# Graph norm and attention on one core: row sums of the attention weights by adding transfers in place of TensorE, with the finishing steps put in other places

## The chip, the cores and the metric

The kernel runs on one core of one Trainium2 chip. The metric is device time in microseconds; before the change it is 2455.19 us, the median of three runs (2455.09 to 2455.25). All data is float32.

## What is computed

Two layers. The first is a graph convolution with two matrix products and batch norms; the second is an attention whose queries come from a graph product and whose keys and values come from the rows themselves. The change touches the end of the second layer only: the softmax's denominators and what divides by them.

```python
# layer 1, cut (x: 16 batches of 1024 rows of 256; h = 4 heads of hd = 64)
Wg = adj[None, :, :] * A_s                              # A_s from the rows' means
g = jnp.einsum('bcn,bnm->bcm', fea, Wg)
g = jax.nn.relu(g * para.reshape(1, C, N))
q = jnp.transpose(g, (0, 2, 1)).reshape(B, N, h, hd).transpose(0, 2, 1, 3)
kv = (x @ kv_w).reshape(B, N, 2, h, hd).transpose(2, 0, 3, 1, 4)
k, v = (kv[0], kv[1])
attn = jax.nn.softmax(jnp.einsum('bhnd,bhmd->bhnm', q, k) * scale, axis=-1)
out = jnp.einsum('bhnm,bhmd->bhnd', attn, v)
# ...
x = _layernorm(x + out, axis=-1)
```

The kernel takes the softmax apart: it computes the exponentials e of the scores without a maximum, sums e times v over the keys, sums e over the keys for the denominator, and divides at the very end, when the rows are finished.

## The kernel before

The kernel computes the attention in steps. A step is two blocks of 128 keys for one pair of heads and one half (512) of the queries. Four steps make a turn: one pair, one half of a batch. Four turns make a batch, in the order half 0 pair 0, half 0 pair 1, half 1 pair 0, half 1 pair 1. In each step TensorE makes the scores of the step after, ScalarE the exponentials, VectorE adds them to a running sum, and TensorE multiplies them with the values.

```python
def exps(g):
    for a in range(2):
        E[g, a] = ep.tile([P, 2, FB], F32, tag="e", name=f"e{g}_{a}")
        nc.scalar.activation(E[g, a], S.pop((g, a)), AF.Exp)

def sums(g):
    b, hf, pair, cp = step(g)
    # ... (the very last step is left to dens)
    if cp == 0:
        ACC[b, hf, pair] = accp.tile([P, 2, FB], F32, tag="acc", name=f"acc{g}")
        nc.vector.tensor_add(ACC[b, hf, pair], E[g, 0], E[g, 1])
    else:
        for a in range(2):
            nc.vector.tensor_add(ACC[b, hf, pair], ACC[b, hf, pair], E[g, a])
```

The running sum `acc` has 128 partitions, [128, 2 heads, 512 queries]: each partition holds the sum over every 128th key. What is missing is the sum over the 128 partitions. TensorE makes it after both pairs of a half, by a product with ones, 32 output rows a head, all alike. ScalarE copies the result, and eight rows a head go to a buffer in DRAM beside the heads' outputs:

```python
DR = 8
CD = C + HEADS * DR
# ...
accp = right("accp", 2)
# ...
def dens(b, hf):
    p = ps_t.tile([P, FB], F32, tag="t", name="pd")
    for pair in range(NP):
        acc = ACC.pop((b, hf, pair))
        for h in range(2):
            k = 32 * (2 * pair + h)
            more = EX.get((b, hf, pair), [])
            for n, t in enumerate(more + [acc]):
                nc.tensor.matmul(
                    p[k : k + 32, :], ones32, t[:, h, :], start=n == 0, stop=n == len(more)
                )
    DT[b, hf] = otp.tile([P, FB], F32, tag="dt", bufs=1, name=f"dt{b}_{hf}")
    nc.scalar.copy(DT[b, hf], p)
    if not by_pe(b, hf):
        for k in range(HEADS):
            put_o(b, hf, slice(C + k * DR, C + (k + 1) * DR), DT[b, hf][32 * k : 32 * k + DR, :])
```

The buffer is read back in blocks of 32 rows (`fetch_o`), VectorE transposes these blocks, and so has for each query its 256 outputs and its four denominators in one partition:

```python
def finish_a(b, j):
    # ... (the last half of the last batch takes another way: by_pe)
        t = pool_r[0].tile([P, 2, CD], F32, tag=pool_r[1], name=f"r_{b}_{j}")
        nc.vector.transpose(
            t.rearrange("p a c -> p (a c)"), OB.pop((b, j)).rearrange("p a c -> p (a c)")
        )
        nc.vector.reciprocal(rd, t[:, :, C:].rearrange("p a (h r) -> p a h r", r=DR)[:, :, :, 0])
        p = r = t[:, :, :C]
    # ... times rd, plus the rows of before, mean and variance (VectorE),
    # ... the norm's factors (GpSimd); finish_b applies them (ScalarE) and stores
```

One `finish_a` covers 256 queries, so a half has two and a batch four (j = 0 to 3). The pieces that are not steps are put into the turns by a table: `put(b, t, f, ...)` places f ahead of the steps of turn t // 2 of batch b (t may run on into the next batch), `between` places it after a given step. Within a turn they are ordered by rank:

```python
order = (dens, recips, x1_t, finish_a, fetch_o, finish_b, x1_v, rows, ln1_a, ln1_b, put_x1, get_x1, means, load, crow)
```

`bn2_q` (GpSimd) scales a later batch's fetched rows, `rows` transposes them and adds (VectorE), `ln1_a` takes their mean and variance (VectorE, then GpSimd), `ln1_b` applies the norm (ScalarE), and `x1_v` transposes the normed rows once more (VectorE); `keys`, `values` and `graph` are products on TensorE for the next batch, and `gate` makes the graph's weights (ScalarE, VectorE). The first sum of a turn stands behind the last of the turn's short pieces of TensorE, `dens` among them:

```python
behind = max((k + 1 for k, fa in enumerate(now) if is_short(fa)), default=0)
```

Of the kernel before, what the change touches and what calls it, by code (L numbers as in the profile page):

```python
# [9 lines left out]
F32 = mybir.dt.float32  # L10
AF = mybir.ActivationFunctionType
OP = mybir.AluOpType
# [4 lines left out]
P = 128  # L17
# [5 lines left out]
def gnn_norm_attention_kernel(  # L23
# [59 lines left out]
    y_blk = [yT_all[b].rearrange("i (d e) (q n) -> q e (i d) n", e=Q, q=NQ) for b in range(B)]  # L83


    DR = 8
    CD = C + HEADS * DR
    o_dram = {(b, h): dram.tile([NT // NH, CD, P], F32, name=f"o{b}_{h}") for b in range(B) for h in range(NH)}
    x1_dram = {
# [39 lines left out]
    with ExitStack() as l0:  # L129
# [280 lines left out]
        right = lambda name, bufs: ctx.enter_context(tc.tile_pool(name=name, bufs=bufs, side="right"))  # L410
        keep = right("keep", 1)
        ldp = right("ldp", LDP)
        accp = right("accp", 2)
        RD = keep.tile([P, B * NT + 1, HEADS], F32, name="RD")
        ones32 = keep.tile([P, 32], F32, name="ones32")
        stq = keep.tile([P, 2, C // Q], F32, name="stq")
# [164 lines left out]
    def fast():  # L581
      with ExitStack() as fx:
# [245 lines left out]
        def by_pe(b, hf):  # L828
            return b == B - 1 and hf == NH - 1

        def attend(g):
            b, hf, pair, cp = step(g)
            if cp == 0:
                O[b, hf, pair] = [ps_t.tile([P, FB], F32, tag="t", name=f"o{g}_{r}") for r in range(2)]
            for a in range(2):
                cb = 2 * cp + a
                for r in range(2):
                    for h in range(2):
                        nc.tensor.matmul(  # L839
                            O[b, hf, pair][r][h * HD : (h + 1) * HD, :],  # L840
                            vs[b][r * HD : (r + 1) * HD, cb, pair * P + h * HD : pair * P + (h + 1) * HD],
                            E[g, a][r * HD : (r + 1) * HD, h, :],
                            start=(cb == 0),
                            stop=(cb == NT - 1),
                        )
# [65 lines left out]
        def finish_a(b, j):  # L911
            hf, k = divmod(2 * j, KB)
            pool_r = (rp, "r") if b < B - 1 or not by_pe(b, hf) else (x1p, "x1")
            rd = RD[:, b * NT + 2 * j : b * NT + 2 * j + 2, :]
            if by_pe(b, hf):
                r = pool_r[0].tile([P, 2, C], F32, tag=pool_r[1], name=f"r_{b}_{j}")
                p = OB.pop((b, j))
            else:
                t = pool_r[0].tile([P, 2, CD], F32, tag=pool_r[1], name=f"r_{b}_{j}")
                nc.vector.transpose(  # L920
                    t.rearrange("p a c -> p (a c)"), OB.pop((b, j)).rearrange("p a c -> p (a c)")
                )
                nc.vector.reciprocal(rd, t[:, :, C:].rearrange("p a (h r) -> p a h r", r=DR)[:, :, :, 0])
                p = r = t[:, :, :C]
            if j == NT // 2 - 1 and by_pe(b, hf):

                for a in range(2):
                    for h in range(HEADS):
                        nc.scalar.mul(r[:, a, ts(h, HD)], p[:, a, ts(h, HD)], rd[:, a, h : h + 1])
            else:  # L930
                nc.vector.tensor_mul(
                    r.rearrange("p a (h d) -> p a h d", h=HEADS),
                    p.rearrange("p a (h d) -> p a h d", h=HEADS),
                    rd.unsqueeze(3).to_broadcast([P, 2, HEADS, HD]),
                )
            nc.vector.tensor_add(r, r, x1s.pop((b, j)))
            mv, rs = ln_stats(sm, r, f"z{b}_{j}")
            nm = sm.tile([P, 2], F32, tag="nm", name=f"nm_{b}_{j}")
            for a in range(2):
                nc.gpsimd.tensor_scalar(  # L940
                    nm[:, a : a + 1], mv[:, a, 0:1], rs[:, a : a + 1], -1.0, op0=OP.mult, op1=OP.mult
                )
            R[b, j] = (r, rs, nm)

        def finish_b(b, j):
            r, rs, nm = R.pop((b, j))
# [46 lines left out]
        for b in range(B):  # L993

            for hf in range(NH):
                t = (hf + 1) * (NC // NH)
                put(b, t, dens, b, hf)
                if by_pe(b, hf):
                    put(b, t, recips, b, hf)
                for k in range(KB // 2):  # L1000
                    j = hf * (KB // 2) + k

                    if b * NH + hf < B * NH - 3:
                        t_f, t_a, t_b = (t + 1, t + 2 + k, t + 6 + k) if hf == 0 else (t + 1, t + 4 + k, t + 6 + k)
                    elif not by_pe(b, hf):

                        t_f, t_a, t_b = t, t + 2 * k, t + 2 + 2 * k if b < B - 1 else (t + 2, NC + 1)[k]
                        if b == B - 1 and k == 0:
                            between[(b * NC + t_b) * 2 + NK // 2] = [(finish_b, (b, j))]
                            t_b = None  # L1010
                    else:
                        t_f, t_a, t_b = t, t + 1 + k, t + 2 + k
                    put(b, t_f, back if by_pe(b, hf) else fetch_o, b, j)
                    if t_a == t:
                        between[(b * NC + t) * 2 + NK // 2] = [(finish_a, (b, j))]
                    else:
                        put(b, t_a, finish_a, b, j)
                    if t_b is not None:
                        put(b, t_b, finish_b, b, j)
            if b == 0:  # L1020
                continue

            if b > 1:
                put(b - 2, 2, begin, b)
                for j in range(NT // 2):
                    put(b - 2, j, load, b, j)
                    put(b - 2, j + 1, bn2_q, b, j)
                    put(b - 2, j + 2, rows, b, j)
                    put(b - 2, j + 2, ln1_a, b, j)
                    put(b - 2, j + 3, ln1_b, b, j)  # L1030
                    put(b - 2, j + 3, put_x1, b, j)
                    put(b - 2, 5 + j // 2 * 2, get_x1, b, j)
                    put(b - 2, min(6 + j, NC), x1_v, b, j)
                put(b - 2, NC - 2, means, b)
                put(b - 2, NC - 1, crow, b)

            i = 0
            for t, n in enumerate(WG):
                for i in range(i, i + n):
                    put(b - 1, t, gate, b, i)  # L1040
# [15 lines left out]
        nsteps = B * NS  # L1056


        order = (dens, recips, x1_t, finish_a, fetch_o, finish_b, x1_v, rows, ln1_a, ln1_b, put_x1, get_x1, means, load, crow)
        rank = {f: k for k, f in enumerate(order)}  # L1060
        short = (dens, recips, x1_t, back)

# [15 lines left out]
        def arrange(pieces):  # L1078
            first = []
            gates = [fa for fa in pieces if fa[0] is gate]  # L1080
            many = [fa for fa in pieces if fa[0] in long]
            first += [fa for fa in pieces if fa[0] is bn2_q]
            alone = [fa for fa in pieces if fa[0] in (dens, back, recips, crow)]
            few = [fa for fa in pieces if fa not in first + gates + many + alone]
# [119 lines left out]
        for t in range(-NC // 2, max(max(at) // 2, nsteps // NK - 1) + 1):  # L1204
            g = NK * t
            now = [p for s in (2 * t, 2 * t + 1) for p in [(opening, (s,))] + arrange(at.get(s, []))]
            behind = max((k + 1 for k, fa in enumerate(now) if is_short(fa)), default=0)
            for k in range(len(now) + 1):
                if k == behind and 0 <= g < nsteps:
                    sums(g)  # L1210
                if k < len(now):
                    f, a = now[k]
                    f(*a)
            for k in range(g, g + NK):
                if 0 <= k + 1 < nsteps:
# [174 lines left out]
```

## Time and profile before

| | before |
|---|---|
| time, median of three | 2455.19 us |
| span of the profiled execution | 2454.0 us |
| column sums on TensorE (L870, over `acc`) | 256 instructions, 36.1 us busy |
| ScalarE's copy of them (L874) | 32, 0.586 us each in the median |
| running sums on VectorE (L824) | 382, 1333 ns each |
| transposes of fetched outputs (L920) | 62, 768 ns each |
| GpSimd's scaling of rows (L624) | 120, 1544 ns each |
| transfers | 292.73 MB, 583951 packets, 407528 of them under 512 B |

In the profile, PE is TensorE's matmul, PEld its loading of weights, DVE VectorE, ACT ScalarE, POOL GpSimd and SPq the queue from which transfers are issued. L870 is line 870 of the kernel. A float32 matmul of the program shows as two instructions. The names tell what is written and read: `pd<-acc,ones` is the column sum, `ot<-o,ot` the end of a pair's output, `r<-ob` the transpose of a fetched piece, `e<-s` the exponentials, `yt<-yt,stq` the scaling of rows. In a row of the order of time, the first two numbers are start and length in microseconds, and in square brackets stands how long the engine sat idle before, and for whom. In a row of a group, after the count, stand the busy time in us, the mean length of one in ns, and the idle time before them with what ended it.

### The profile page before, as it was taken

The numbers are of one execution on the slowest core, as the hardware profiler recorded it, in microseconds if no ns is written. First come the engines' busy times: TensorE is split into PE (matmuls) and PEld (weight loads), VectorE is DVE, ScalarE is ACT, GpSimd is POOL, SyncE is SP. The second block draws the span as 40 slices with busy tenths as digits, with TensorE's granted clock in tenths as the row PEclk, the third lists the DMA queues.
The fourth block names the chain that finished last, engine by engine and source line by source line (L and its number), as shares of the span: only waits on it lengthen the run. The fifth ranks groups of instructions, "written<-read, shape, count | busy, mean of one in ns | idle before, by whom it ended". The sixth has DMA issues, their size and how long they took to land. (4 is left out here: it accounts for less than half of the span.)

```text
span 2454.0 us, 33894 instructions
## 1 busy us (share of the span) xinstructions
PE 2411.8 (98%) x12225; PEld 1008.5 (41%) x12225; DVE 1811.3 (74%) x2584; ACT 1094.8 (45%) x1555; POOL 776.9 (32%) x826
## 2 busy tenths in 40 slices
PE   8999999999999899999999999999999999999997
PEld 4444444444344443443434434344343443443432
DVE  5555545556776777888788888888888888888677
ACT  2000000001554455564655646656566565564645
POOL 2222222231556521414224133232332323414013
PEclk9999999999999899999999999999999999999999
DMA  3122122222578543544545545545354453544222
GB/s 137 69 86 103 69 86 103 85 87 86 199 272 278 133 121 83 143 119 112 143 106 129 143 95 146 122 120 144 81 150 114 123 149 89 145 112 118 72 44 56
DMA packets 583951, 292.73 MB, mean 119 GB/s; under 512 B 407528, under 2 KB 556512, under 8 KB 576608
## 3 DMA queue, kind: packets, MB, share of 16 engines
q1 hardware_dynamic: 583776, 290.49, 43.0%
q8 instruction: 98, 1.61, 0.3%
q14 instruction: 77, 0.63, 0.1%
HBM read 194.46 MB, written 95.94 MB: 118 GB/s over the span
## 5 line engine op out<-in xcount | busy, mean ns | idle before, releaser
L809 ACT ACTIVATE e<-s 128x1024 f32<-128x1024 f32 x512 | 496.0, 1020 | 327.5 <-PE s L797 265.4
L824 DVE TENSOR_TENSOR acc<-acc,e 128x1024 f32<-128x1024 f32 x382 | 509.3, 1333 | 112.1 <-ACT e L809 85.4
L797 PE MATMUL s<-qT,kT 64*64 64x512 f32 x4096 | 490.7, 594 | 4.4 <-ACT e L809 1.7
L839 PE MATMUL o<-e,v 64*64 64x512 f32 x4096 | 485.3, 589 | 0.0
L771 PE MATMUL pg<-wg,x 128*128 128x512 f32 x960 | 426.5, 597 | 0.0
L624 POOL TENSOR_TENSOR yt<-yt,stq 128x512 f32<-128x512 f32 x120 | 185.2, 1544 | 406.4 <-DMA yt<-yT 239.8
L771 PEld LDWEIGHTS pg<-wg,x 128*128 128x128 f32 x960 | 178.7, 190 | 238.6 <-issue 237.4
L839 PEld LDWEIGHTS o<-e,v 64*64 64x64 f32 x4096 | 156.6, 133 | 282.9 <-issue 275.2
L797 PEld LDWEIGHTS s<-qT,kT 64*64 64x64 f32 x4096 | 147.1, 133 | 298.5 <-issue 254.2
L107 ACT COPY u<-pa 128x512 f32<-128x512 f32 x15 | 8.8, 586 | 475.3 <-PE pa L313 475.3
L66 POOL TENSOR_SCALAR rs_z<-mv_z 128x2 f32<-128x2 f32 x64 | 18.5, 290 | 470.5 <-DVE mv_z L573 470.4
L730 DVE SCALAR_TENSOR_TENSOR wg<-wg,adj 128x1024 f32<-128x1024 f32 x128 | 163.4, 1308 | 2.8
L313 PE MATMUL pa<-AhT,x 128*128 128x512 f32 x360 | 161.8, 592 | 0.0
L656 ACT ACTIVATE x<-x,nm_a,rs_a 128x256 f32<-128x256 f32 x128 | 75.8, 594 | 171.9 <-POOL nm_a L646 171.4
L851 DVE TENSOR_TENSOR ot<-o,ot 128x512 f32<-128x512 f32 x64 | 44.2, 691 | 127.5 <-ACT ot L850 127.5
L757 PE MATMUL pv<-kvw,x1T 128*128 128x256 f32 x512 | 118.7, 385 | 0.0
L746 PE MATMUL pk<-x1T,kvw 128*128 128x512 f32 x256 | 117.9, 604 | 0.0
L66 POOL TENSOR_SCALAR rs_a<-mv_a 128x2 f32<-128x2 f32 x64 | 38.0, 594 | 236.5 <-DVE mv_a L573 235.2
L344 PE MATMUL ph<-agg,SW 128*128 128x512 f32 x240 | 112.8, 592 | 0.0
L757 PEld LDWEIGHTS pv<-kvw,x1T 128*128 128x128 f32 x512 | 97.1, 192 | 31.8 <-issue 16.2
L313 PE MATMUL pa<-T,sx 128*128 128x512 f32 x240 | 107.9, 592 | 0.0
L313 PEld LDWEIGHTS pa<-AhT,x 128*128 128x128 f32 x360 | 68.4, 190 | 86.1 <-issue 86.1
(198 smaller groups left out, 3147.1 us busy)
## 6 DMA issues: line engine op xcount, KB each, us to landing
adj<-in_adj_dram SPq DMA_DIRECT2D x128, 512.0 KB
h<-hT SPq DMA_DIRECT2D x28, 1024.0 KB
hL<-h SPq DMA_DIRECT2D x28, 1024.0 KB
ob<-o SPq DMA_DIRECT2D x248, 72.0 KB
x<-in_x_dram SPq DMA_DIRECT2D x16, 1024.0 KB
yT<-y SPq DMA_DIRECT2D x64, 256.0 KB
out_dram<-r SPq DMA_DIRECT2D x64, 256.0 KB
xr<-in_x_dram SPq DMA_DIRECT2D x62, 256.0 KB
```

The costliest lines, as they stand in the source:

```text
L313: nc.tensor.matmul(p, xs[n][:, k, :], bs[n][:, k, :], start=(k == 0), stop=(k == KN - 1))
L344: nc.tensor.matmul(p, ws[n][:, ts(f, P)], bs[n], start=True, stop=True)
L624: nc.gpsimd.tensor_tensor(y, y, sc, op)
L656: nc.scalar.activation(r, r, AF.Identity, bias=nm[:, a : a + 1], scale=rs[:, a : a + 1], accum_out=css[b][:, i : i + 1])
L730: nc.vector.scalar_tensor_tensor(t, t, 1.0, adjs[b * NT + i], op0=OP.add, op1=OP.mult)
L746: nc.tensor.matmul(p, kvw[:, k, ts(c, P)], x1Ts[b][:, k, ts(h, FB)], start=(k == 0), stop=(k == CT - 1))
L757: nc.tensor.matmul(p[:, ts(a, C)], x1Ts[b][:, k, ts(j + a, P)], kvw[:, k, C:], start=(k == 0), stop=(k == CT - 1),)
L771: nc.tensor.matmul(pg[b], x1s[b, k // 2][:, k % 2, ts(c, P)], wgs[b, k][:, ts(h, FB)], start=(k == 0), stop=(k == NT - 1))
L797: nc.tensor.matmul(t[r * HD : (r + 1) * HD, h, :], kTs[b, pair][h * HD : (h + 1) * HD, ts(2 * cb + r, HD)], qTs[b, pair, hf][h * HD : (h + ...
L809: nc.scalar.activation(E[g, a], S.pop((g, a)), AF.Exp)
L824: nc.vector.tensor_add(ACC[b, hf, pair], ACC[b, hf, pair], E[g, a])
L839: nc.tensor.matmul(O[b, hf, pair][r][h * HD : (h + 1) * HD, :], vs[b][r * HD : (r + 1) * HD, cb, pair * P + h * HD : pair * P + (h + 1) * HD],
```

## The change

In all half batches but the last three, the sum over the partitions is no longer made by TensorE. Two transfers issued by GpSimd add instead: the first adds partitions 64 to 127 of `acc` to partitions 0 to 63, the second adds 32 to 63 to 0 to 31. The 32 rows that remain, each a sum over every 32nd key, go to DRAM (so 32 rows a head in place of eight), and after the transpose VectorE sums these 32 numbers for each query. The aim is to take the column sums off TensorE and their copy off ScalarE.

For this the running sums get a third buffer, and the pieces are placed anew. The folds stand at the front of the turn after their pair; `put_den` follows within that turn. The second piece of half 1 (`finish_late`) stands behind `ln1_a`, the statistics of later rows; other finishing steps go between steps. Since `dens` no longer holds back the first sum of a turn, a batch's first sum is put behind the transposes of the rows (`x1_v`), which the keys of that turn read. The diff, cut to its core:

```diff
-    DR = 8
+    DR = Q                                   # Q = 32
-        accp = right("accp", 2)
+        accp = right("accp", 3)
+        def by_dma(b, hf):
+            return b * NH + hf < B * NH - 3
+
+        def fold(b, hf, pair, n):
+            acc = ACC[b, hf, pair]
+            nc.gpsimd.dma_start(acc[:n], acc[n : 2 * n], accum_op=OP.add)
+
+        def put_den(b, hf, pair):
+            acc = ACC.pop((b, hf, pair))
+            for h in range(2):
+                r = C + (2 * pair + h) * DR
+                put_o(b, hf, slice(r, r + DR), acc[:DR, h, :])
 ...
-                t = pool_r[0].tile([P, 2, CD], F32, tag=pool_r[1], name=f"r_{b}_{j}")
-                nc.vector.transpose(
-                    t.rearrange("p a c -> p (a c)"), OB.pop((b, j)).rearrange("p a c -> p (a c)")
-                )
-                nc.vector.reciprocal(rd, t[:, :, C:].rearrange("p a (h r) -> p a h r", r=DR)[:, :, :, 0])
-                p = r = t[:, :, :C]
+                p = r = pool_r[0].tile([P, 2, C], F32, tag=pool_r[1], name=f"r_{b}_{j}")
+                den = otp.tile([P, 2, CD - C], F32, tag="den", bufs=1, name=f"den_{b}_{j}")
+                ob = OB.pop((b, j))
+                nc.vector.transpose(den, ob[:, :, C:])
+                nc.vector.transpose(r, ob[:, :, :C])
+                den = den.rearrange("p a (h r) -> p a h r", r=DR)
+                if by_dma(b, hf):
+                    nc.vector.tensor_reduce(rd, den, AX.X, OP.add)
+                    nc.vector.reciprocal(rd, rd)
+                else:
+                    nc.vector.reciprocal(rd, den[:, :, :, 0])
 ...
-                put(b, t, dens, b, hf)
+                if by_dma(b, hf):
+                    for pair in range(NP):
+                        s = b * NC + t + 2 * (pair - NP + 1)
+                        for k in range(2):
+                            put(0, s + k, fold, b, hf, pair, P // 2 >> k)
+                        between.setdefault(2 * s + 2, []).append((put_den, (b, hf, pair)))
+                else:
+                    put(b, t, dens, b, hf)
 ...
                     if b * NH + hf < B * NH - 3:
-                        t_f, t_a, t_b = (t + 1, t + 2 + k, t + 6 + k) if hf == 0 else (t + 1, t + 4 + k, t + 6 + k)
+                        t_f, t_a, t_b = t + 2 + k * hf, t + 3 + hf, t + 6 + k
+                        if k != hf:
+                            t_a = None
+                            between.setdefault((b * NC + t + 2) * 2 + hf, []).append((finish_a, (b, j)))
+                        if hf == 1 and k == 0:
+                            t_f = None
+                            between.setdefault((b * NC + t) * 2 + NK - 1, []).append((fetch_o, (b, j)))
 ...
-                        put(b, t_a, finish_a, b, j)
+                        put(b, t_a, finish_late if by_dma(b, hf) and hf == 1 else finish_a, b, j)
 ...
-        order = (dens, recips, x1_t, finish_a, fetch_o, finish_b, x1_v, rows, ln1_a, ln1_b, put_x1, ...)
+        order = (dens, recips, x1_t, put_den, finish_a, fetch_o, finish_b, x1_v, rows, ln1_a, finish_late, ln1_b, put_x1, ...)
+            first += [fa for fa in pieces if fa[0] is fold]
             first += [fa for fa in pieces if fa[0] is bn2_q]
 ...
-            behind = max((k + 1 for k, fa in enumerate(now) if is_short(fa)), default=0)
+            opens = lambda fa: is_short(fa) or (fa[0] is x1_v and g % NS == 0)
+            behind = max((k + 1 for k, fa in enumerate(now) if opens(fa)), default=0)
```

More of the change, by code (lines that the diff above doesn't have):

```diff
@@ L943, in finish_a, with finish_late @@
             R[b, j] = (r, rs, nm)
+        def finish_late(b, j):
+            finish_a(b, j)
         def finish_b(b, j):
@@ L1008, in fast @@
                         if b == B - 1 and k == 0:
-                            between[(b * NC + t_b) * 2 + NK // 2] = [(finish_b, (b, j))]
+                            between.setdefault((b * NC + t_b) * 2 + NK // 2, []).append((finish_b, (b, j)))
                             t_b = None
@@ L1012, in fast @@
                         t_f, t_a, t_b = t, t + 1 + k, t + 2 + k
-                    put(b, t_f, back if by_pe(b, hf) else fetch_o, b, j)
+                    if t_f is not None:
+                        put(b, t_f, back if by_pe(b, hf) else fetch_o, b, j)
                     if t_a == t:
-                        between[(b * NC + t) * 2 + NK // 2] = [(finish_a, (b, j))]
-                    else:
-                        put(b, t_a, finish_a, b, j)
+                        between.setdefault((b * NC + t) * 2 + NK // 2, []).append((finish_a, (b, j)))
+                    elif t_a is not None:
+                        put(b, t_a, finish_late if by_dma(b, hf) and hf == 1 else finish_a, b, j)
                     if t_b is not None:
@@ L1056, in fast @@
         nsteps = B * NS
-        order = (dens, recips, x1_t, finish_a, fetch_o, finish_b, x1_v, rows, ln1_a, ln1_b, put_x1, get_x1, means, load, crow)
+        order = (dens, recips, x1_t, put_den, finish_a, fetch_o, finish_b, x1_v, rows, ln1_a, finish_late, ln1_b, put_x1, get_x1, means, load, crow)
         rank = {f: k for k, f in enumerate(order)}
```

## The prediction

> **What bounds the kernel now.** I read the page's first part, then the order of time on TensorE through two turns of one batch in the steady part, then the busy time of the four turns, then VectorE's groups, and last what ScalarE waits for in the turn that is tightest. A turn is one head pair of one half batch: four steps of scores, exponentials and weighted values, with the products for later batches ahead of them. A batch has four turns, numbered 0 to 3.
>
> The page's first part:
>
> ```profile
> PE 2411.8 (98%) x12225; PEld 1008.5 (41%) x12225; DVE 1811.3 (74%) x2584; ACT 1094.8 (45%) x1555; POOL 776.9 (32%) x826
> ```
>
> TensorE is nearly never empty, but 98% alone could hide waits, because overlapping matmuls count as busy. So I look at when its groups start. In order of time, the beginning of turn 2 and of turn 3 of the same batch (start, length, engine, line, count):
>
> ```profile
> 1526.13 1.12 PE L771 MATMUL pg<-wg,x 128*128 128x512 f32 x2
> 1527.19 1.07 PE L870 MATMUL pd<-acc,ones 128*32 128x512 f32 x8
> 1528.18 7.99 PE L771 MATMUL pg<-wg,x 128*128 128x512 f32 x18
> 1536.11 1.95 PE L797 MATMUL s<-qT,kT 64*64 64x512 f32 x16
> ...
> 1550.00 10.57 PE L771 MATMUL pg<-wg,x 128*128 128x512 f32 x24
> 1560.40 0.27 PE L706 MATMUL pc<-ident,cs 128*8 128x128 f32 x1
> 1560.61 1.95 PE L797 MATMUL s<-qT,kT 64*64 64x512 f32 x16
> ```
>
> The start of each group follows the work of the one before without a hole: 24 product instructions take 10.40 us, 0.433 each, and steps repeat every 3.43 us through both turns. TensorE is the bound, and what it no longer does comes off the time, as long as nobody becomes late.
>
> These lines also price what the change removes. Turn 2 runs from 1526.13 to 1536.11, 9.98 us, with 20 product instructions and the eight column sums of L870 between them. Twenty at 0.433 are 8.67, and a switch to another kind of tile costs about 0.1 (the first product after a switch has a record of 697 ns, the others 592). So the eight cost 9.98 - 8.77, about 1.2 us: more than the 1.07 of their record, because they switch the array twice.
>
> **What the Trainium skill says.** "TensorEngine Tiling (Array Packing)", Key Properties, says that changing the tiling mode drains TensorE. The trace agrees in kind and gives the size, about 0.1 us a switch. "DMA: Bandwidth & Descriptors", SWDGE vs HWDGE vs iDMA, says that accumulation in a transfer goes only through GpSimd's queue; its section on the anatomy of such a transfer fits about 2.0 us plus bytes over 436 GB/s. An estimate from that page is 2.6 us for the first fold (256 KB) and 2.3 us for the second (128 KB), before any queueing; no run here shows one. "SBUF — State Buffer", Who interferes with whom, says that a VectorE instruction with two SBUF inputs contends with a GpSimd instruction that reads SBUF. The trace agrees: the running sum takes 1.19 us at best, 1.225 in the median, and up to 2.1 us; in turn 1, beside GpSimd's scaling of rows, four of them took 6.52 us.
>
> **The change, part by part.** Removed: in 29 of 32 half batches (all with b*2+hf under 29) the eight TensorE instructions, and ScalarE's copy of their result (0.586 us, L874). TensorE: 29 x 1.2 = 34.8 us, and all of it lies on the path, since TensorE has no hole there. The only regular hole that I find is about 0.2 to 0.3 us in turn 0 of each batch (the third group of scores waits for ScalarE, which is still at the gates); ScalarE loses its copy there, so this hole should not grow.
>
> Added on GpSimd: four accumulating transfers per half batch, two per pair, each with an issue. The first waits for the last running sum of its pair; the second for the landing of the first. GpSimd is busy 31.8 of 100.5 us in a batch, so time is there; order matters more, because the scaling of rows (two of 1.54 us) now stands behind the fold.
>
> Added on VectorE, per fetched pair of row tiles:
>
> ```profile
> L920 DVE STREAM_TRANSPOSE r<-ob 128x576 f32<-128x576 f32 x62 | 47.6, 768 | 2.0 <-DMA ob<-o 2.0
> L628 DVE STREAM_TRANSPOSE x<-yt 128x512 f32<-128x512 f32 x60 | 42.5, 709 | 3.6 <-POOL yt L624 2.2 <-POOL rs_z L66 0.4
> L213 DVE TENSOR_REDUCE row<-A 128x1 f32<-128x1024 f32 x4 | 4.9, 1214 | 0.0
> ```
>
> One transpose of 576 columns becomes one of 512 (709 ns) and one of 256. The two rows above give 59 ns per 64 columns, so 256 columns take 709 - 236, about 470 ns: together 1.18 us for 0.77, +0.41. The sum over 32 rows reads 256 elements; scaled from 1214 ns for 1024 with some fixed part, about 0.4. So +0.8 us for each of 58 finishes, 46 us in all, 3.2 us per batch.
>
> Added to the transfers: denominators grow from 8 to 32 rows a head (64 KB instead of 16 KB, four per half), the fetch from 72 to 96 KB a piece (eight per half), and 384 KB of folding per pair. The four turns below have DMA shares of 0.34 to 0.70, so this fits, but it lengthens landings.
>
> Moved: the finishing of half 1's first piece goes from turn 2 to the middle of turn 1 of the next batch; the second piece's stands in turn 2 behind the statistics of the next rows; both of half 0 stay in turn 3, one at its start and one after its first step.
>
> **Does VectorE or ScalarE become late?** Busy time by turn (turn 0, 1, 2, 3):
>
> ```profile
> 1474.70:1499.00 24.30, 24.17 (x162) 9.34 (x162) 20.28 (x19) 18.65 (x23) 6.96 (x4) 1.00 0.70 168
> 1499.00:1526.90 27.90, 27.90 (x172) 12.70 (x171) 23.22 (x28) 17.27 (x25) 11.19 (x12) 1.00 0.54 151
> 1526.90:1550.70 23.80, 23.80 (x157) 8.75 (x157) 21.81 (x38) 11.30 (x19) 9.48 (x16) 1.00 0.44 85
> 1550.70:1575.20 24.50, 24.50 (x154) 9.36 (x154) 19.52 (x32) 11.74 (x19) 4.11 (x8) 1.00 0.34 87
> ```
>
> The columns are length, then PE, PEld, DVE, ACT and POOL busy. VectorE has 84.8 of 100.5 us, 84%. After the change it has about 88.0 of 98.1, 90%. One finish is 3.7 us now (1527.46 to 1531.12) and about 4.5 after. Turn 1 gets one: 23.2 + 4.5 = 27.7 in 27.9, just full, and there VectorE idles 2.1 us before it can start its second step's sums, so it ends some 1 to 2 us late. Turn 2 loses two and gets one: 21.8 - 7.4 + 4.5 = 18.9 in 22.6, where the lateness is made up. Turn 3: 19.5 + 1.6 = 21.1 in 24.5. Turn 0: unchanged, 20.3 in 23.1. Six buffers of weights, three steps of 3.43 us, stand between VectorE and ScalarE, so 1 to 2 us do not reach TensorE.
>
> The tight place is ScalarE's in turn 2:
>
> ```profile
> 1536.73 0.60 ACT L656 ACTIVATE x<-x,nm_a,rs_a 128x256 f32<-128x256 f32 x1 [7.80 <-POOL nm_a L646]
> ...
> 1538.05 1.92 ACT L809 ACTIVATE e<-s 128x1024 f32<-128x1024 f32 x2
> ```
>
> Its exponentials stand behind the norm of rows, which waits for GpSimd, which waits for VectorE's sums. TensorE needs the first score buffer back at 1539.59 and gets it at 1539.07: 0.5 us to spare. Without the eight instructions TensorE comes 1.2 us earlier, so this chain has to be 0.7 us earlier too. The change sees to that: 3.7 us of finishing leave the front of it, against up to 2 us of lateness from turn 1 and the scaling of rows now behind a fold. I expect it just to hold, or to cost a few tenths.
>
> So the sum is 2455.2 - 34.8 = 2420.4 if nothing is late. I allow 0.25 us for each of 14 batches, 3.6 us, and choose 2424.
>
> **Rivals.**
> First: VectorE becomes the bound, or hands lateness on from turn to turn. For it: 90%, and a fetch for the first piece of turn 3 that is issued only at that turn's start, when its landing takes about 2 to 4 us. Against it: each turn still has slack by the table. One microsecond per batch would give 2435; three, about 2463.
> Second: GpSimd's queue. The fold at the front of a turn holds back the scaling of rows and the norm's small operations, and ScalarE's exponentials wait with them. For it: the 0.5 us above. Against it: 68% of GpSimd's time is idle. It would give 2430 to 2445.
> Third: the folds land late, since they share the 16 engines with 128-byte packets; then the fetches and finishes slip. There are some 12 us between a pair's first fold and the put that reads it, against an estimate of 5 to 8 us for two. If it does not hold, 2440 or more.
> Fourth: the sums were hidden anyway, and nothing is gained. The gapless starts speak against it.
>
> **Range and chances.** The floor is 2420.4, and the small hole in turn 0 could give another 2 us: low end 2418. Lateness is the only way to lose, and it comes in units of 14 us per microsecond in a batch, so the upper side is longer: 2441. A gain over 2% would need 48 us, more than is removed: 0.02. A loss over 2% needs 6 us of lateness per batch: 0.05. The rest is 0.93.
>
> **What would show it.** Right: 24 instructions of L870 instead of 256 over acc, turns 0 and 2 of a batch about 1.2 us shorter each, turns 1 and 3 unchanged, VectorE near 90% in the steady part, and no wait of TensorE's scores or values. Wrong: scores that wait for exponentials at the start of turn 2 or 3, keys that wait for the transposed rows in turn 0, a transpose of fetched rows that idles for its transfer, or a score group that starts more than 3.43 us after the one before.

## The result and the profile after

The changed kernel takes 2438.75 us (median of four runs, 2435.90 to 2439.42); the kernel before, on the same chip, 2455.22 (2455.09 to 2455.83). The ratio is 0.993, with a 95% interval of 0.9913 to 0.9947: a gain of 16.5 us, which lies inside the range of the prediction and 14.75 us above its centre. TensorE lost the work that the prediction counted. About half of the 34.8 us that it counted was lost again in three places, only one of which was in the prediction.

The page's first part, after:

```profile
PE 2382.2 (98%) x11993; PEld 1005.8 (41%) x11993; DVE 1832.6 (75%) x2704; ACT 1081.0 (44%) x1526; POOL 880.6 (36%) x942
```

TensorE has 232 instructions fewer (29 halves by eight) and 29.6 us less of busy time; GpSimd has 116 instructions more, the folds. The share of 98% is the same as before, so again only the order of time tells where TensorE waits. The answer to the stretch shown for before, turn 2 and the start of turn 3 on TensorE (start, length, engine, line, count):

```profile
1911.37 8.85 PE L771 MATMUL pg<-wg,x 128*128 128x512 f32 x20
1920.15 1.95 PE L797 MATMUL s<-qT,kT 64*64 64x512 f32 x16
...
1934.05 10.57 PE L771 MATMUL pg<-wg,x 128*128 128x512 f32 x24
```

Turn 2 now runs from its first product to its first scores in 8.78 us instead of 9.98: the column sums between the products are gone, with their two switches, and nothing took their place. The busy time of the four turns (0, 1, 2, 3; columns as before: length, PE, PEld, DVE, ACT, POOL busy, granted clock, share of the transfers, GB/s):

```profile
2155.60:2179.20 23.60, 23.19 (x156) 8.98 (x152) 21.01 (x20) 18.27 (x21) 6.71 (x6) 1.00 0.75 170
2179.20:2207.10 27.90, 27.90 (x177) 13.08 (x173) 24.07 (x37) 17.23 (x24) 12.41 (x17) 1.00 0.82 197
2207.10:2229.80 22.70, 22.70 (x153) 8.54 (x149) 21.64 (x33) 10.80 (x17) 11.79 (x17) 1.00 0.44 82
2229.80:2254.30 24.50, 24.50 (x158) 9.36 (x154) 19.42 (x36) 11.73 (x18) 8.16 (x10) 1.00 0.71 141
```

Turns 1, 2 and 3 have no hole. Turn 0 has holes of 0.4 us together: 23.19 busy of 23.60. VectorE has 86.1 of 98.7 us, 87%.

If the starts of TensorE's turns are measured through the whole trace, the account is this. The spans of the two profiled executions are 2454.0 and 2437.5, 16.5 apart, so the account can be closed (differences in us):

| where | before | after | difference |
|---|---|---|---|
| steady turns 1, 2, 3 | 27.86, 23.87, 24.50 | 27.86, 22.67, 24.50 | 15 turns 2: -17.90 |
| turn 0 of the next batch, mean of 14 | 24.30 | 23.68 (23.10 to 25.11) | -8.65, where 14 x 1.2 would be -16.8 |
| second turn of the last batch | 15.70 | 19.24 | +3.54 |
| last product of weighted values to the end | 18.48 | 24.70 | +6.22, of which 5.03 after ScalarE's last operation |
| the rest | | | +0.26 |

So 26.6 of the 34.8 us arrived in the steady part, and 9.8 were given back at the end. Each of these is followed below.

**The hole in turn 0.** The batch that lost most (turn 0 of 25.11 us) shows it best. The second half of its key products on TensorE, and the transposed rows that they read, on VectorE:

```profile
1863.87 3.67 PE L746 MATMUL pk<-x1T,kvw 128*128 128x512 f32 x8 [1.77 <-ACT wg L720]
```

```profile
1862.43 1.29 DVE L679 STREAM_TRANSPOSE x1T<-xb 128x512 f32<-128x512 f32 x2
```

The row names ScalarE's gates wg, but ScalarE had ended those at 1861.2; the rows x1T end at 1863.72, and the keys start 0.15 us later. In other batches the same wait is put down to x1T by name. Measured from start to start, and against the run with the earlier fetch below, the key products lost 7.9 us in 10 turns, nearly all that turn 0 lost against its shortest. So what was VectorE late for? Its groups, with the idle time before them and what ended it:

```profile
L939 DVE STREAM_TRANSPOSE r<-ob 128x512 f32<-128x512 f32 x62 | 41.4, 668 | 0.0
L938 DVE STREAM_TRANSPOSE den<-ob 128x256 f32<-128x256 f32 x62 | 27.3, 440 | 61.1 <-DMA ob<-o 60.7 <-issue 0.3
L942 DVE TENSOR_REDUCE RD<-den 128x8 f32<-128x256 f32 x58 | 21.8, 375 | 0.0
```

The means are as the prediction sized it: 0.44, 0.67 and 0.38 us. But the first transpose sat idle for 60.7 us until a fetched piece had landed, against 2.0 in the kernel before. In order of time it is in turn 3 of each batch; in the one whose turn 3 begins at 1934.05:

```profile
1942.27 0.45 DVE L938 STREAM_TRANSPOSE den<-ob 128x256 f32<-128x256 f32 x1 [3.26 <-DMA ob<-o]
```

and the queue that issues the fetch, in the same turn:

```profile
1935.98 6.09 SPq L922 DMA_DIRECT2D ob<-o  x8
```

The fetch of the first piece of half 0 goes out from 1935.98 on, right behind the last put of that half (1935.49), and VectorE has nothing it may do between 1939.0 and 1942.27. In the kernel before, the same fetch went out in turn 2, 18 us before turn 3 began (at 1550.0), and the first transpose of turn 3 followed VectorE's work without idle time. First the queue, then VectorE:

```profile
1531.86 5.68 SPq L906 DMA_DIRECT2D ob<-o  x8
```

```profile
1552.46 0.77 DVE L920 STREAM_TRANSPOSE r<-ob 128x576 f32<-128x576 f32 x1
```

So the change itself moved this fetch a turn later: it has to follow `put_den`, which now stands after the third step of turn 2, and it was put at the start of the next turn.

**The last batch.** Its second turn has one hole on TensorE and, in the same stretch, ScalarE's wait for GpSimd's norm factors; the exponentials stand behind that norm. First TensorE, then ScalarE:

```profile
2374.22 2.74 PE L797 MATMUL s<-qT,kT 64*64 64x512 f32 x16 [3.53 <-ACT e L809]
```

```profile
2371.19 2.07 ACT L973 ACTIVATE r<-r,nm,rs_z 128x256 f32<-128x256 f32 x4 [2.32 <-POOL nm L961]
2373.17 1.91 ACT L809 ACTIVATE e<-s 128x1024 f32<-128x1024 f32 x2
```

In the kernel before the same two waits are 1.68 and 0.47 us; on TensorE:

```profile
2398.66 2.00 PE L797 MATMUL s<-qT,kT 64*64 64x512 f32 x16 [1.68 <-ACT e L809]
```

And after the change TensorE does not come back at full speed. Windows before, in and after the 5.2 us that follow the hole (the granted clock is the number before the last two):

```profile
2370.00:2374.20 4.20, 0.69 (x8) 0.00 (x0) 3.99 (x9) 3.01 (x6) 1.39 (x2) 1.00 0.59 188
2374.20:2379.40 5.20, 5.18 (x32) 1.64 (x36) 4.85 (x7) 2.92 (x3) 4.28 (x4) 0.67 0.16 53
2379.40:2384.00 4.60, 4.60 (x48) 1.68 (x44) 2.74 (x3) 1.95 (x3) 0.56 (x1) 1.00 0.00 0
```

32 instructions run in a stretch that holds 48 at the full clock. So 1.85 us of more waiting became 3.5 of lost time.

**The end.** Between ScalarE's last operation and the end of the span lie 4.86 us before and 9.89 after. GpSimd's closing drain, from the rows of the program's last line (minimum, median and maximum of the durations in ns), before:

```profile
L1385 POOLq DRAIN  x3: 34/50/82, 2449.0 to 2453.7; - x3
```

and after:

```profile
L1429 POOLq DRAIN  x3: 34/98/9538, 2427.2 to 2437.3; - x3
```

One of the three drains, the first, takes 9.54 us, from 2427.2 on; the first of before took 0.05, and the longest 0.08.

### The profile page after: what moved, and what is told of

The parts are those of the page before. It is cut to its first block, busy times and chain, and to the rows that moved or that the text cites. A ratio compares the mean times of both kernels' runs of the same rounds, so it can differ in the third digit from the quotient of the medians.

```text
span 2437.5 us, 33793 instructions
## 1 busy us (share of the span) xinstructions
PE 2382.2 (98%) x11993; PEld 1005.8 (41%) x11993; DVE 1832.6 (75%) x2704; ACT 1081.0 (44%) x1526; POOL 880.6 (36%) x942
## 5 line engine op out<-in xcount | busy, mean ns | idle before, releaser
L824 DVE TENSOR_TENSOR acc<-acc,e 128x1024 f32<-128x1024 f32 x382 | 479.8, 1256 | 78.5 <-ACT e L809 47.9
L839 POOL DMA_DIRECT2D acc<-acc x116 | 99.5, 857 | 393.8 <-DVE acc L824 282.9
L624 POOL TENSOR_TENSOR yt<-yt,stq 128x512 f32<-128x512 f32 x120 | 173.1, 1443 | 92.7 <-DMA yt<-yT 77.7
L66 POOL TENSOR_SCALAR rs_z<-mv_z 128x2 f32<-128x2 f32 x64 | 41.1, 642 | 326.1 <-DVE mv_z L573 289.8
L313 PEld LDWEIGHTS pa<-AhT,x 128*128 128x128 f32 x360 | 68.4, 190 | 86.1 <-issue 86.1
L821 DVE TENSOR_TENSOR acc<-e,e 128x1024 f32<-128x1024 f32 x64 | 98.9, 1545 | 1.2 <-ACT e L809 1.2
```

The lines of the kernel that those rows point to most:

```text
L313: nc.tensor.matmul(p, xs[n][:, k, :], bs[n][:, k, :], start=(k == 0), stop=(k == KN - 1))
L624: nc.gpsimd.tensor_tensor(y, y, sc, op)
L839: nc.gpsimd.dma_start(acc[:n], acc[n : 2 * n], accum_op=OP.add)
```

## The experiments

The first theory on turn 0, called the landing theory here, was that the fetch leaves too late for its landing; its rival was that VectorE simply has more work. Other questions followed from the account: what the folds add to that landing, which parts of the rearrangement are needed, what makes the last batch late, and what the drain counts. All edits are made in the changed kernel, whose 2438.75 us they are to be read against; ratios are against the kernel before on the same chip, with 95% intervals.

| run | time, us | ratio to before | interval |
|---|---|---|---|
| the change | 2438.75 | 0.993 | 0.9913 to 0.9947 |
| fetch one step earlier | 2430.08 | 0.9897 | 0.9881 to 0.9914 |
| eight rows where nothing is folded | 2434.96 | 0.9916 | 0.9899 to 0.9932 |
| no fold | 2458.16 | 1.0009 | 1.0000 to 1.0018 |
| first sum ahead of the transposes | 2452.77 | 0.9990 | 0.9983 to 0.9997 |
| folds in one half only | 2458.32 (one run) | | |
| the late finish not late | 2486.76 | 1.0131 | 1.0114 to 1.0148 |
| fetch earlier, one norm later | 2424.48 | 0.9874 | 0.9858 to 0.9891 |
| these and eight rows | 2423.51 | 0.9870 | 0.9854 to 0.9886 |
| the same, with a drain in the last batch | 2419.99 | 0.9856 | 0.9839 to 0.9872 |
| two buffers of running sums | 2434.69 | 0.9918 | 0.9901 to 0.9934 |

### The fetch one step earlier

```diff
+                        if hf == 0:
+                            t_f = None
+                            between.setdefault((b * NC + t) * 2 + NK - 2, []).append((fetch_o, (b, j)))
                         if hf == 1 and k == 0:
                             t_f = None
```

> The changed kernel, but half 0's two fetches are issued after the third step of turn 2, right behind the put of the folded rows, not at the start of turn 3. Theory L (landing: VectorE waits in turn 3 for the first fetched piece, 3.1 to 5.3 us, and what it loses there makes the rows' last transposes late, for which the keys of turn 0 wait): the idle time before that transpose falls below 1 us, turn 0 takes 23.1 us in all 14 batches instead of 23.68 in the mean, so about 8 us less than the changed kernel: 2430.5. Rival V (VectorE is late from its sheer load of some 90%): the fetch is not what it lacks, turn 0 stays at 23.4 us or more, the time at 2436 to 2439.

Measured 2430.08 us. All 14 turns 0 are now 23.10 or 23.11 us. What VectorE's first transpose waits for, in this run:

```profile
  DMA ob<-o: 2.5, 2
```

The key products of the turn that had lost most are one group again:

```profile
1852.46 7.13 PE L746 MATMUL pk<-x1T,kvw 128*128 128x512 f32 x16
```

The work of VectorE is the same, only the fetch has moved, and the hole is gone: the landing theory holds and the rival falls. The hole was worth 8.1 us (14 x 0.58), and the time fell by 8.7. One step is enough.

Within the trace of the change the relation can be read too. Up to a wait of about 3.3 us turn 0 is at its floor (3.10 to 3.26 us give 23.10 to 23.12), and above it follows the wait one to one: 3.56 gives 23.34, 4.10 gives 23.89, 5.33 gives 25.11.

### No fold, with everything else as changed

```diff
         def by_dma(b, hf):
-            return b * NH + hf < B * NH - 3
+            return False
```

The places of the finishing steps stay as changed, `finish_late` too; TensorE makes the column sums again, and 32 rows a head go to DRAM.

> The changed kernel's placement, wider rows and third buffer, but no adding transfers: TensorE makes the column sums in every half batch. Theory (the placement costs nothing where TensorE has the column sums; the folds alone lengthen the end): turns 2 and 0 of a batch take 23.9 and 24.3 us again, the time from ScalarE's last operation to the end is 4.9 us as before the change and not 9.9, and the whole is 2455.2 + 3.5 for the last batch, 2458 to 2460. Rival (the placement itself costs): 2463 or more, with turns longer than before the change. Rival on the end (it is longer for another reason than GpSimd's queue of transfers): 9.9 us stays.

Measured 2458.16 us, and turns of 23.87 to 24.08 and 24.30 where the folds give 22.67 and 23.10. So the new order and the wider fetch alone bring no gain (the time is 2.65 us above that of the kernel before); the gain is the column sums. The 3.5 us expected for the last batch were too many: its second turn takes 16.69, 1.0 above before, and TensorE keeps its clock after a hole of 2.67 us. The drain is back at 0.05 us and the end at 5.13. The fetched pieces are waited for here as well:

```profile
  DMA ob<-o: 35.5, 17
```

In turn 3 that is 2.2 us in the mean of 14 batches (1.9 to 2.9), all below the 3.3 at which it begins to cost. With folds it is 3.9. In both runs the fetch goes out 1.9 us into the turn and VectorE is ready for it 4.9 us into it, in every batch; the transpose can start at 6.8 to 7.8 us without folds and at 8.0 to 10.2 with them. So the wait has two parts: about 2.2 us by the place of the fetch, and about 1.7 by the folds, since both folds of the next pair are under way at that time. Neither crosses the threshold alone: this run has the place without the folds, the run before it the folds without the place.

### A batch's first sum ahead of the rows' transposes

```diff
-            opens = lambda fa: is_short(fa) or (fa[0] is x1_v and g % NS == 0)
+            opens = is_short
```

> The changed kernel without its last part: a batch's first sum of weights stands ahead of the rows' transposes again. Theory L and V alike: the transposes come 1.2 to 1.5 us later in each of 14 batches, the keys wait that much longer, 17 to 21 us in all: 2455 to 2460, so this part alone would decide between a gain and none. Rival: the keys have room after all, and the whole stays within 2 us of 2438.7.

Measured 2452.77 us. Turns 1, 2 and 3 stay as they are; turn 0 becomes 24.38 to 26.97 us, and the key products lose 27.4 us by their starts (the profiled execution took 2457.51 us, more than the median). In two of the 14 turns the clock was halved behind the hole as well. What the key products wait for in this run:

```profile
  DVE x1T L679: 19.1, 13
```

The first sum is some 1.2 us or more of VectorE ahead of the transposes. So this small part of the change carries 14 us; without it nearly all of the gain is lost. It is also the same road on which the fetch's lateness reached TensorE.

### The late finish not late

```diff
-                        put(b, t_a, finish_late if by_dma(b, hf) and hf == 1 else finish_a, b, j)
+                        put(b, t_a, finish_a, b, j)
```

> The changed kernel without finish_late: half 1's second piece is finished ahead of the rows' statistics in turn 2 again. Theory (ScalarE's norm of rows stands ahead of its exponentials and waits for those statistics; it has about 1.5 us to spare): a finish of 4.4 us ahead makes turn 2 some 2.9 us longer in each of 14 batches, 40 us in all: 2470 to 2482, slower than the kernel before. Rival (VectorE's order does not matter in turn 2): 2438 to 2441.

Measured 2486.76 us, 48.0 above the change. Turn 2 takes 26.7 to 27.1 us instead of 22.67 in 13 batches, turns 0 are nearly all at 23.10. A finish ahead of the statistics of the next rows puts ScalarE's norm, and the exponentials behind it, later. TensorE in one of those turns:

```profile
1958.58 3.39 PE L797 MATMUL s<-qT,kT 64*64 64x512 f32 x16 [2.53 <-ACT e L809]
1961.80 1.89 PE L855 MATMUL o<-e,v 64*64 64x512 f32 x16
```

The hole is 2.5 us, and the 16 instructions behind it take 3.2 us from their start to the next group's, where 1.7 to 1.8 is usual. So 2.5 of the 4.3 us are the wait and most of the rest is the clock. The direction was expected, the size was not: what was left out of it is the half clock. The prediction had this chain as its tight place; the run shows that the order chosen in the change is what keeps it from failing.

### Eight rows where nothing is folded

The last three halves are not folded, but the change has them carry 32 rows a head all the same. Here they keep eight, and a fetched piece of theirs has 288 columns instead of 384:

```diff
-    CD = C + HEADS * DR
+    den_rows = lambda b, h: DR if b * NH + h < B * NH - 3 else 8
+    # puts, fetches and the transpose of den use den_rows(b, hf) rows a head
```

> The changed kernel, but the half batches that still use TensorE's column sums put and fetch eight rows a head again, as before the change. Theory W (the second turn of the last batch lost 3.5 us because the wider rows made its fetch land later): that turn goes from 19.2 back to about 15.7 us, the whole to 2435.2. Rival (VectorE's second transpose, 0.35 us a finish, makes it late): it stays within 1 us of 19.2, and the whole within 1 us of 2438.7.

Measured 2434.96 us. The second turn of the last batch is 18.17 us, not the 15.7 of before: TensorE's hole is 2.70 us instead of 3.53. Neither guess holds. In the five other traces with folds, 32 rows and the norm in its old place this hole is 3.10 to 3.53 us long, so the width makes 0.4 to 0.8 us of the lateness, and not all of it. The length of the turn says less, because the half clock comes and goes (17.11 to 20.05 us in those five). The interval overlaps that of the change: of the 4.3 us between the two profiled spans 1.1 lie in this turn, 1.3 in turns 0 and 1.5 behind the last product, where no effect of the edit is shown.

### One norm later in the last batch

What ScalarE waits for in the hole are the factors for the norm of the third piece of batch 14. The kernel already has a place for such a norm between the steps, used for the last batch alone. Added to the earlier fetch:

```diff
-                        if b == B - 1 and k == 0:
+                        if k == 0:
                             between.setdefault((b * NC + t_b) * 2 + NK // 2, []).append((finish_b, (b, j)))
```

> The run with the earlier fetch, and besides the norm of batch 14's third piece is applied after the third step of the last batch's second turn instead of ahead of its steps. Theory C (that turn is long because ScalarE waits for this norm's factors with the exponentials behind it, TensorE idles over 3 us, and then its clock is halved for some 3 us: granted clock 0.56 and 0.67 in such stretches): neither idle time nor half clock, the turn takes 14.0 us instead of 20.0, the whole 2424. Rival (the clock drops for another reason): the idle 3.3 us go, the half clock stays, the turn takes 16 to 17 us, the whole 2427.

Measured 2424.48 us. The second turn takes 14.13 us, without a hole, and the turn after it 16.16 instead of 14.89; against the earlier fetch alone (20.05 and 14.89) the two together fell by 4.7, the time by 5.6. So the cause of the hole is settled: four operations of norms in a row ahead of the exponentials, of which the last two had no factors yet.

### These three together

The earlier fetch, the later norm and the eight rows:

> The three steps together: earlier fetch of half 0, eight rows a head where TensorE makes the column sums, and the later norm in the last batch. With the norm out of the way the narrower rows have nothing left to shorten: within 1 us of the run without them, 2424. If width mattered elsewhere: 2422 or less.

Measured 2423.51 us. The turn after the second is back at 14.89. The intervals overlap that of the run above, but the four times of each do not (2423.22 to 2423.84 against 2424.33 to 2424.79), and the traces put 1.3 us into this turn: so about 1 us is the likely worth of the narrower rows here, more than the theory gave them. The drain at the end is still 9.54 us.

### Folds in one half only

The drain's price could be a fixed one, for having used such transfers at all, or one for each transfer. Only half 0 of batch 0 is folded here, four transfers in place of 116; the other halves have their column sums on TensorE.

```diff
-            return b * NH + hf < B * NH - 3
+            return b * NH + hf < 1
```

> As the run without adding transfers, but the very first half batch folds: 4 such transfers in all, the last of them 1400 us before the end. Theory F (the end is longer by a fixed price for having used GpSimd's queue of transfers at all: its closing DRAIN takes 9.54 us with 116 of them, 0.05 with none): the DRAIN takes 9.5 us again, the time from ScalarE's last operation to the end is 9.9 us, the whole about 2462. Rival (the DRAIN grows with the number of transfers): about 0.4 us, an end of 5 us, the whole about 2457.

One run, 2458.32 us. Its closing drains:

```profile
L1429 POOLq DRAIN  x3: 34/98/392, 2451.1 to 2456.2; - x3
```

So 0.05 us for no transfer, 0.39 for four, 9.54 for 116: about 82 ns for each (9.49 / 116; 0.34 / 4 gives 86), and no fixed price. In all eight traces that close with 116 such transfers, the change's among them, it is 9.54. All of them are of the same two sizes, so a price for each transfer and one for each packet can't be told apart. At four the end stays at 5.16 us, since the rest of the closing takes about 5 us anyway; only what is longer than that lies on the path.

### A drain where GpSimd has nothing to do

If the price is for each transfer since the last drain, it can be paid earlier. The version with all three edits gets one line more:

```diff
+        between.setdefault((B - 1) * NS + 3, []).append((lambda: nc.gpsimd.drain(), ()))
```

> Theory P (what GpSimd's closing drain takes, 9.54 us after 116 adding transfers, is a piece of work for each transfer since the last drain, here 82 ns each): a drain put into the last batch, after the last such transfer and in 16.6 us in which GpSimd has nothing to do, takes these 9.5 us there, off the path; the closing one takes about 0.05 to 0.4 us, the end after ScalarE's last operation falls from 9.9 to about 5.1 us, and the time from 2423.5 to about 2418.8. Rival Q (the closing drain costs by what the program has sent in all, or waits for the rings themselves to be taken down): the added drain is short or long, the closing one stays at 9.5 us, and the time stays at 2423.5 within 1 us.

The added drain, and the closing ones of the same run:

```profile
L1259 POOLq DRAIN  x1: 11162/11162/11162, 2358.4 to 2358.4; - x1
```

```profile
L1443 POOLq DRAIN  x3: 34/41/98, 2410.7 to 2416.3; - x3
```

The price moved: 11.2 us in the last batch (9.5 were expected; the 1.7 more are not explained), 0.04 at the end, and the end after ScalarE's last operation is 5.4 us instead of 9.9. The expected place was a gap of 16.6 us; in fact the drain fell behind a norm's factors, from 2358.4 on, and made the next ones 4 to 6 us late, but ScalarE's norm had that time, and the turns of the last batch are those of the run without it. Measured 2419.99 us where 2418.8 was expected. The medians differ by 3.5 us and their intervals overlap; the 4.5 us at the end are read from the traces. This is the fastest version of the study, 18.8 us below the change.

### Two buffers of running sums instead of three

```diff
-        accp = right("accp", 3)
+        accp = right("accp", 2)
```

> The changed kernel with two buffers for the running sums, as before the change, in place of three. Theory: a pair's sum is free again when its 32 rows have gone to DRAM, within the turn after it, so a third buffer is used only for a short while and two do nearly as well: 2438.75 within 1.5 us, and no wait of VectorE's first sum of a turn for a transfer. Rival: folds take 8 to 10 us and the put follows them, so that the first sum of the turn after next waits for it: turns longer by 1 us or more, 2450 or above.

Measured 2434.69 us, with the same turns 1, 2 and 3 as the change and turns 0 of 23.10 to 24.23 (mean 23.57). VectorE's first sums wait for no transfer. So the third buffer does nothing here, and the rival falls. That it came out 4 us below the change, more than the theory allowed, is not an effect of the buffers that any view shows. In its trace 2.1 us lie in the second turn of the last batch (17.11; a hole of 3.10 us was there, and the clock stayed whole), 1.6 in turns 0, and 2.2 before the attention begins, which the edit doesn't touch. The intervals overlap.

## Why the prediction was right in its range and too low in its centre

**TensorE's saving: right.** The prediction had 29 x 1.2 = 34.8 us, all on the path. In the change 26.6 of it show; with the fetch one step earlier, the steady part, from the end of the first batch's turn 0 to the end of batch 14, takes 1448.84 us where before took 1483.47: 34.6 less. 24 column sums are left (now L886), turn 2 is 1.19 shorter in all 15 batches, turns 1 and 3 are unchanged. The rest of the account is what takes away from this.

**VectorE's added work: right.** 0.44 + 0.67 + 0.38 = 1.49 us in place of 0.77, +0.72 a finish against +0.8. The share of 90% was a little high (87% in the batch shown). By turn the table was further off: 27.7 us were forecast for turn 1 and 18.9 for turn 2, and the batch shown has 24.07 and 21.64. The running sums themselves shifted: those over two new inputs (L821) went from 1212 to 1545 ns in the mean, and the others (L824) from 1333 to 1256. The scaling of rows on GpSimd now lies beside the first sum of turn 2, which takes 2.86 us at 1912.70 with the scaling from 1913.15 to 1916.47. That agrees with what the prediction took from "SBUF — State Buffer".

**Turns 1 and 2 and the tight place: right.** No wait of TensorE there, and ScalarE's exponentials no longer stand late behind the norm of rows:

```profile
1921.37 1.94 ACT L809 ACTIVATE e<-s 128x1024 f32<-128x1024 f32 x2 [0.26 <-PE s L797]
```

They wait 0.26 us for their scores; before, they had to wait for the norm. The reason given was the right one too: with a finish put back in front (the run with the late finish not late), this is where 4.3 us a turn are lost.

**GpSimd's queue and the folds' landing: no loss, but not for the reason given.** From the view of the transfers (KB each, and the median us from issue to landing), the two folds of a pair:

```profile
acc<-acc POOLq DMA_DIRECT2D x58, 256.0 KB, 4.4
acc<-acc POOLq DMA_DIRECT2D x58, 128.0 KB, 3.9
```

The estimates from "DMA: Bandwidth & Descriptors" were 2.6 and 2.3 us, before any queueing; 0.86 us of each is the issue itself. In turn 2 of nearly every batch the queue comes on top: after the first fold GpSimd scales rows and makes the factors of norms, and the second fold stands behind all of that, 11.8 us after the first.

```profile
1912.48 0.91 POOL L839 DMA_DIRECT2D acc<-acc  x1 [0.25 <-DVE acc L824]
1924.28 0.84 POOL L839 DMA_DIRECT2D acc<-acc  x1
```

It has landed 15.1 us after the first one's issue. So "5 to 8 us" for two in "some 12" did not hold there: in 12 of the 15 turns 2 the put of these rows went out within 0.1 us of that landing, so it had waited for it. This cost nothing, since the fetch of these rows went out only at the start of turn 3, and even the earlier fetch left turn 0 at its shortest. That the folds lengthen another landing, by about 1.7 us, is the part of this rival that mattered.

**The allowance of 0.25 us for each of 14 batches: this step failed.** It measured 0.58, 8.1 us instead of 3.6. The prediction's first rival named the cause, "a fetch for the first piece of turn 3 that is issued only at that turn's start, when its landing takes about 2 to 4 us", and then set it aside since "each turn still has slack by the table". The slack of turn 3 is real (19.42 busy of 24.50), but it can't be used while the engine waits for a transfer and its instructions stand in order. The transpose idled 3.1 to 5.3 us in each batch. About 3.3 of these were taken up on the way; what was above came out as keys waiting for transposed rows in turn 0. Both are signs that the prediction had listed as showing it wrong. What it had not read is that the kernel before made this fetch a turn earlier, so that the wait was new and came from the change.

**The last batch and the end: not in the sum.** The prediction scaled one batch by 14 or 29 and put nothing from the program's last 100 us into the sum. There 3.5 us came from the norm that wasn't ready plus the half clock, and 5.0 from the drain. Together 8.5 us, more than half of the miss of 14.75. Turn 0 makes 8.1 - 3.6 = 4.5, and the rest (1.2 between the last product and ScalarE's last operation, of which three other runs show 0.7 to 0.8 and the rest at most 0.1, and small shifts) is not explained. So the time lay in the range partly by luck: the upper side was kept for lateness in the batches, and more than half of what filled it came from places that the prediction had not counted.

## What to carry to other kernels

When work is put where an engine has slack by busy time, look at what its first instruction there waits for: an engine in order can't spend slack that lies behind a wait, so ask where the change moves a fetch, and place it by the landing it will have with the new traffic, not by the one of the old profile. Read the last turns and the closing of the program as a stage of their own, since they don't repeat what the steady part shows. Adding transfers through GpSimd's queue have a second bill here, at the next drain, and one can choose where it is paid.

## What was not expected of the hardware

- GpSimd's drain takes time for each of its adding transfers since the last drain, about 82 ns, though in the changed kernel the last of them was issued 113 us before: 0.05, 0.39 and 9.54 us for 0, 4 and 116, and an added drain takes it over.
- A short hole on TensorE can cost 1.3 to 2.7 us more by a half clock behind it, but not always. "TensorE: Matmul & The Clock Gate" of the Trainium skill, Part 1: The HAM clock gate, What's actually happening, says that the clock is halved after an idle window of about 3.4 us, in windows that run freely. Here the length of the hole doesn't decide, and shorter holes are enough: holes of 2.1 to 2.8 us had the half clock behind them in all 13 batches of the run without the late finish (16 instructions in 3.1 to 3.5 us instead of 1.8), while holes of 2.67 (no fold), 3.10 (two buffers) and 3.18 us (first sum ahead) in the last batch had none. In the run with the first sum ahead, holes of 1.91 and 1.93 us before key products had it, and one of 2.02 had not. Whether the place of a hole in such a window decides wasn't tested.
